# Letting a group's row gathers go on two by two, paced by TensorE's products (graph network layer, one core)

## The chip, the cores and the metric

The kernel runs on one core of one Trainium2 chip. The metric is the device time of one execution in microseconds (us), lower is better. Engines are named as the profile names them: PE is TensorE, DVE VectorE, ACT ScalarE, POOL GpSimd, SP SyncE (it only issues DMAs here).

## What is computed

One message-passing layer of a graph network with a residual and two layer norms: 6250 nodes with 128 features, 100000 edges sorted by destination, 4 attributes an edge.

```python
msg_in = concat([x[src], x[dst], edge_attr], axis=1)     # 100000 x 260
h = silu(msg_in @ mW1 + mb1)
aggregated = segment_sum(h @ mW2 + mb2, dst, num_segments=6250)
u = silu(concat([x, aggregated], axis=1) @ uW1 + ub1)
x = layernorm(x + layernorm(x + u @ uW2 + ub2) * ln_g + ln_b)
```

## The kernel before, in words

The product of `msg_in` with `mW1` is split. A table `tab_a` (all nodes times the first 128 rows of `mW1`) is made once and lies in HBM; `tab_b` is the same for the destinations. The edges are cut into 98 groups of 1024 edges, 8 tiles of 128 each. Since the edges are sorted, the destinations of a group lie in a window of 80 nodes.

One step of the main loop (`for g in range(NG)`, L1005) does one group. For most groups (86 of 98, in the list `listed`; a group's place in that list is its turn) the rows `tab_a[src]` are fetched by indirect DMAs, one for each tile of 128 edges, issued by POOL in `fetch` (L210, the DMA is L215). The other 12 groups (14, 21, 28, ... 91, in `by_sort`) need no gather: TensorE picks their rows from a copy of the table in SBUF with 0/1 matrices (`select`, L938), with products and evictions around it (L915, L916, L924, L945, L953, L954) that are spread over the six steps ahead of such a group.

The step of a listed group g issues, in this order:

- POOL: the gathers of the group four turns ahead (`fetch(ahead(g, 4))`). They go into one of 6 buffers `ga`, so they wait until ACT has read the buffer's last user, the group six turns earlier (L582).
- SP: the loads of the group three turns ahead: destinations (`near`), the window of `tab_b` (`mv`), the attributes (`st`).
- DVE, then ACT: `hidden(g)`: the gathered rows plus the product of the destinations' part (L581, reads `ga` and PSUM `pre`), then SiLU into `h` (L582).
- DVE: the 0/1 matrices of the group two turns ahead (L534 and L544).
- PE: `before_rows` of the next turn's group (L566, 8 tiles, into PSUM `pre`), then what a sorted group ahead needs (L915, L938, L953), then `sums(g)`: a small transpose (L588) and 8 tile products `h` times 0/1 matrix that add up in PSUM `pt` (L590).
- DVE: `add`: `pt` is added to the running sums `acc` and `deg` (L611). There is one buffer `pt`, so the next group's sums wait for it.

Each fp32 product stands in the profile as two matmuls and two weight loads, so a group has 16 records of L566 and 16 of L590. The order on every engine is the order in which the code is written; the waits between engines are semaphores that the framework sets from the tiles. POOL does hardly anything but issue gathers: 40 from `x` for the first five groups, which go another way, and 646 from `tab_a`. Every 512 nodes a batch of the node update (L628 to L690) comes between.

Of the kernel before, what the change touches and what calls it, by code (L numbers as in the profile page):

```python
# [25 lines left out]
def kernel(  # L26
# [18 lines left out]
    nc = tc.nc  # L45
# [5 lines left out]
    G = 8  # L51
# [4 lines left out]
    WS = 112  # L56
# [6 lines left out]
    RAW = 5  # L63
    NM = 4
# [19 lines left out]
    listed = [g for g in range(NG) if g not in by_sort]  # L84
# [7 lines left out]
    def turn_of(g):  # L92
        return listed.index(g)
# [4 lines left out]
    def ahead(g, n):  # L98
        i = listed.index(g) + n
        return listed[i] if i < len(listed) else NG  # L100
# [16 lines left out]
    def tiles_of(g):  # L117
        return min(G, TI - g * G)
# [17 lines left out]
    start = ExitStack()  # L136
    first = start.enter_context(tc.tile_pool(name="first", bufs=1, side="right"))

    def wide():
        return ps.tile([P, G, P], F32, name="pre")  # L140

    def narrow():
        return ps1.tile([P, 2 * P], F32, name="pt")
# [62 lines left out]
    sd = dram.tile([4, QN * GE], F16, name="sd")  # L206
    ea_d = dram.tile([ED, NG * GE], F32, name="ea_d")
    rows, bases, near = {}, {}, {}

    def fetch(g):  # L210
        if g >= NG:
            return
        rows[g] = gath.tile([P, G, H], F32, name="ga")
        for i in range(tiles_of(g)):
            nc.gpsimd.indirect_dma_start(  # L215
                out=rows[g][:, i, :],
                out_offset=None,
                in_=x if g < RAW else tab_a[:, :],
                in_offset=bass.IndirectOffsetOnAxis(ap=src_i[:, g, i : i + 1], axis=0),
            )  # L220

    for g in range(RAW - 1):
        fetch(g)
# [8 lines left out]
    pos_i = first.tile([R, P], I32, name="pos_i")  # L232
    nc.gpsimd.iota(pos_i, pattern=[[P, P]], base=0, channel_multiplier=P * P)
    fetch(RAW - 1)

    b1 = bcast("b1", mb1)
# [165 lines left out]
    def turned_first(k):  # L402
        pt = wide()
        if k < 2:
            turned_x(k, pt, node, name="xT", bufs=3)
        else:
            turned_x(k, pt, first, name="xT", bufs=2)
        return pt

    pt = {0: turned_first(0)}  # L410
# [27 lines left out]
    mv = []  # L438
# [89 lines left out]
    oh, pre, xg, h_s = {}, {}, {}, {}  # L528
# [30 lines left out]
    def before_rows(g):  # L559
        if g >= NG:  # L560
            return
        raw = g < RAW
        pre[g] = wide()
        st = stbuf[turn_of(g) % NST].rearrange("k (i c) -> k i c", i=G)
        for i in range(tiles_of(g)):
            nc.tensor.matmul(pre[g][:, i, :], st[:, i, :], mv[turn_of(g) % NM], start=True, stop=not raw)  # L566
            if raw:
                nc.tensor.matmul(
                    pre[g][:, i, :], xg[g][:, i, :], w1[:, 0, :], start=False, stop=True
                )  # L570
        xg.pop(g, None)
# [12 lines left out]
    def sums(g):  # L584
        n = tiles_of(g)
        h, o = h_s.pop(g) if g in h_s else hbuf[turn_of(g) % 2], oh.pop(g)
        pt = narrow()
        nc.tensor.transpose(pt[0:1, P : P + W], deg_g[:, g : g + 1], ident[:W, :W])  # L588
        for i in range(n):
            nc.tensor.matmul(pt[:, :WS], h[:, i, :], o[:, i, :], start=i == 0, stop=i == n - 1)  # L590
        return pt

    acc, deg = {}, {}
# [57 lines left out]
    def inverse(*parts):  # L651
        r = node.tile([P, 2, 2 * BN], F32, name="r")
        lo, hi = parts[0][0], parts[-1][1]
        nc.scalar.activation(r[:, 0, lo:hi], var[:, lo:hi, 1], AF.Sqrt, bias=eps)
        nc.vector.reciprocal(r[:, 0, lo:hi], r[:, 0, lo:hi])
        nc.vector.scalar_tensor_tensor(
            r[:, 1, lo:hi], var[:, lo:hi, 0], -1.0, r[:, 0, lo:hi], op0=OP.mult, op1=OP.mult
        )
        return r

    def scaled(to, v, r, lo, n):
        for i in range(n):
            nc.scalar.activation(  # L663
                to[:, i, :],
                v[:, i, :],
                AF.Identity,
                bias=r[:, 1, lo + i : lo + i + 1],
                scale=r[:, 0, lo + i : lo + i + 1],
            )
# [11 lines left out]
    def node_o(k, r):  # L681
        i0, n = batches[k]
        o = node.tile([P, BN, H], F32, name="o")
        scaled(o, z_sb.pop(k), r, BN, n)
        m = min(i0 + n, nf) - i0
        if m > 0:
            nc.sync.dma_start(
                out[i0 * P : (i0 + m) * P].rearrange("(i p) f -> p i f", p=P), o[:, :m]
            )
        if i0 + n > nf:  # L690
            nc.scalar.dma_start(out[nf * P :], o[: N - nf * P, nf - i0, :])
# [313 lines left out]
    for g in range(NG):  # L1005
# [14 lines left out]
        if g in by_sort:  # L1020
            select(3)
            sorted_hidden()
            turned_hidden(g, 1)
            add(g, sums(g))
            node_stage(g)
            continue
        if g + AHEAD >= RAW:
            fetch(ahead(g, AHEAD))
        if g < RAW:
            if g + 1 < RAW:  # L1030
                turned_rows(g + 1)
            before_rows(g)
# [6 lines left out]
        if g < SORTED:  # L1039
            n = -(-len(todo) // (SORTED - g))  # L1040
# [3 lines left out]
        if g + 1 >= RAW:  # L1044
            before_rows(ahead(g, 1))
        if g == NG - 1:
            node_x(NB - 1)
        sorted_before(g)
        add(g, sums(g))
        sorted_behind(g)  # L1050
        node_stage(g)
    k = NB - 1
    n = batches[k][1]
# [6 lines left out]
    node_o(k - 1, r)  # L1060
    r = inverse((BN, BN + n))
    node_o(k, r)
    edges.close()
    ub2_b, g_b, b_b = late["ub2"], late["g"], late["b"]

# [100 lines left out]
    with tc.If(bad > 0):  # L1166
        with tc.tile_pool(name="all", bufs=1) as whole:
# [11 lines left out]
            with tc.tile_pool(name="turned", bufs=2, space=PSUM) as turned:  # L1179
                for i in range(NT):  # L1180
                    pt = turned.tile([P, P], F32, name="pt")
# [142 lines left out]
```

## Time and profile before

| | before |
|---|---|
| median of 3 runs | 1409.84 us (1408.27 to 1423.03) |
| the profiled execution | 1407.12 us, its span 1405.3 us |
| PE busy | 888.7 us (63%) |
| POOL busy | 657.3 us (47%), 697 instructions |
| DVE busy | 555.5 us (40%) |
| ACT busy | 368.3 us (26%) |
| granted TensorE clock, mean | 0.786 |

In the groups of instructions a row has the line, the engine, the operation, what is written and read, the count, then busy time and mean duration, then the engine's idle time just before these instructions and what ended most of it. "issue" is idle time that no wait in the profile explains. "remote" is a wait that ended with a semaphore's update for which the profile shows no instruction that ended just then. In a timeline a row has start and duration in us, engine, line, operation, and in brackets the idle time before it.

### The profile page before, as it was taken

How to read it: one execution, taken by the hardware profiler on the slowest of the kernel's cores; microseconds unless marked ns; L12 is line 12 of the kernel's file. 1: busy time of each engine (PE TensorE's matmuls, PEld its weight loads, DVE VectorE, ACT ScalarE, POOL GpSimd, SP SyncE). 2: the span in 40 equal slices, each digit the busy share in tenths (PEclk: the TensorE clock that was granted, in tenths of full speed). 3: DMA queues.
4: the chain of work that ended last, by engine and by line, in shares of the span. 5: the costliest groups of instructions: out<-in, count | busy, mean ns of one | idle time of the engine just before them, and what ended most of it. 6: DMA issues, size and time to landing. Idle time of an engine off the chain costs nothing.

```text
span 1405.3 us, 15177 instructions
## 1 busy us (share of the span) xinstructions
PE 888.7 (63%) x5206; PEld 755.8 (54%) x5206; DVE 555.5 (40%) x1287; ACT 368.3 (26%) x518; POOL 657.3 (47%) x697
## 2 busy tenths in 40 slices
PE   3256738577666657647747757667755864864883
PEld 3246736465564545636636646546545653663672
DVE  1056866343432433533423422342443423443353
ACT  1010103231422323313313311232332412331333
POOL 6434455546444464456264354444555446346310
PEclk9977967787777978868767667868879777786895
DMA  6242324322242322332221421324234232132110
GB/s 176 62 134 79 86 66 116 70 74 73 65 98 63 88 74 74 81 81 72 79 75 43 99 71 42 83 65 99 68 91 90 71 97 72 47 98 67 52 50 19
DMA packets 85950, 109.12 MB, mean 78 GB/s; under 512 B 22044, under 2 KB 63152, under 8 KB 85866
## 3 DMA queue, kind: packets, MB, share of 16 engines
q1 hardware_dynamic: 60114, 61.20, 16.3%
q0 software_dynamic: 21952, 45.00, 13.0%
q10 hardware_dynamic: 3800, 1.88, 0.5%
q8 instruction: 43, 0.70, 0.2%
q14 instruction: 41, 0.34, 0.1%
HBM read 96.65 MB, written 11.37 MB: 77 GB/s over the span
## 4 chain that ended last, share of the span: by engine, by line
PE 34%; another core or an unknown queue 21%; DVE 16%; issue 12%; ACT 7%; DMA 1%; DVEq 1%; POOL 0%; SPq 0%; ACTq 0%
PE pt L590 11%; PE po L938 8%; PE pre L566 5%; DVE ga L581 3%; ACT h L582 2%; DVE st L534 2%; PE po L924 2%; ACT pn L663 1%; DVE bn L622 1%; DVE oh L544 1%; PE pn L636 1%; PE pn L635 1%; PE pn L915 1%; PE pn L953 1%
## 5 line engine op out<-in xcount | busy, mean ns | idle before, releaser
L215 POOL DMA_INDIRECT ga<-tab_a,src_i x646 | 617.8, 956 | 668.3 <-ACT h L582 429.6
L590 PE MATMUL pt<-oh,h 128*128 128x112 f32 x1372 | 230.8, 324 | 146.5 <-ACT h L582 76.5
L590 PEld LDWEIGHTS pt<-oh,h 128*128 128x128 f32 x1372 | 207.0, 232 | 176.2 <-ACT h L582 89.4
L566 PE MATMUL pre<-mv,st 128*128 128x128 f32 x1372 | 214.3, 312 | 27.2 <-issue 18.1
L566 PEld LDWEIGHTS pre<-mv,st 128*128 128x128 f32 x1372 | 202.8, 228 | 42.2 <-issue 30.4
L938 PE MATMUL po<-O,A 128*128 128x157 f32 (+47 forms) x1344 | 196.9, 303 | 34.0 <-issue 33.8
L938 PEld LDWEIGHTS po<-O,A 128*128 128x128 f32 x1344 | 191.5, 214 | 38.7 <-issue 38.4
L582 ACT ACTIVATE h<-ga 128x1024 f32<-128x1024 f32 (+1 forms) x81 | 85.4, 1054 | 353.9 <-DVE ga L581 268.3
L611 DVE TENSOR_TENSOR acc<-acc,pt 128x80 f32 x98 | 23.3, 238 | 384.3 <-PE pt L590 190.7
L534 DVE TENSOR_SCALAR_CACHE_REDUCE st<-near,base_p 80x1024 f32<-80x1024 int32 x86 | 109.0, 1268 | 1.4 <-DMA near<-in_dst_dram 0.8
L581 DVE TENSOR_TENSOR ga<-ga,pre 128x1024 f32<-128x1024 f32 (+1 forms) x81 | 98.3, 1214 | 10.3 <-issue 9.9
L904 ACT ACTIVATE O<-sc,p_less 128x512 f32<-128x512 f16 x96 | 63.5, 709 | 94.9 <-remote 44.8
L916 DVE SCALAR_TENSOR_TENSOR st_s<-ar,part,pn 32x512 f32<-32x512 f16 x24 | 18.1, 756 | 171.3 <-remote 117.5
L924 PE MATMUL po<-st_s,mv_s 128*128 128x512 f32 x48 | 34.5, 808 | 76.1 <-DVE st_s L916 58.6
L544 DVE TENSOR_TENSOR oh<-w_row,rel 128x640 f32<-128x640 f32 x86 | 69.9, 813 | 0.0
L900 DVE TENSOR_SCALAR O<-sc,p_rows 128x512 f32<-128x512 f16 x96 | 44.9, 509 | 44.5 <-remote 32.3
L945 ACT ACTIVATE hT<-po 128x512 f32<-128x512 f32 x24 | 14.3, 594 | 168.8 <-remote 81.3
L905 ACT ACTIVATE O<-O,ones 128x1024 f32<-128x1024 f32 x48 | 55.1, 1149 | 1.6
L924 PEld LDWEIGHTS po<-st_s,mv_s 128*128 128x128 f32 x48 | 9.7, 253 | 81.2 <-DVE st_s L916 62.3
L953 PE MATMUL pn<-ident,hT 128*128 128x128 f32 x96 | 18.8, 328 | 51.5 <-ACT hT L945 35.3
L215 POOL DMA_INDIRECT ga<-in_x_dram,src_i x40 | 37.9, 948 | 14.7 <-issue 11.7
L915 PE MATMUL pn<-Oc,at_s 128*128 128x512 f32 x48 | 33.1, 771 | 16.9 <-issue 9.2
(193 smaller groups left out, 806.6 us busy)
## 6 DMA issues: line engine op xcount, KB each, us to landing
near<-in_dst_dram SPq DMA_DIRECT2D x85, 320.0 KB
ga<-tab_a,src_i POOLq DMA_INDIRECT x646
sc<-sd SPq DMA_DIRECT2D x12, 512.0 KB
mv<-tab_b SPq DMA_DIRECT2D x86, 40.0 KB
tab_a<-A SPq DMA_DIRECT2D x11, 256.0 KB
tab_b<-o SPq DMA_DIRECT2D x11, 256.0 KB
out_dram<-o SPq DMA_DIRECT2D x11, 256.0 KB
x<-in_x_dram SPq DMA_DIRECT2D x10, 256.0 KB
```

Source lines behind the costliest of these rows:

```text
L215: nc.gpsimd.indirect_dma_start(out=rows[g][:, i, :], out_offset=None, in_=x if g < RAW else tab_a[:, :], in_offset=bass.IndirectOffsetOnAx ...
L534: nc.vector.tensor_scalar(stbuf[turn_of(g) % NST][:W], near.pop(g), base_p[:W, g : g + 1], 0.0, op0=OP.is_equal, op1=OP.add, accum_out=deg ...
L544: nc.vector.tensor_tensor(oh[g][:, :n, :W], w_row[:, None, :].to_broadcast([P, n, W]), rel[:, g, :n, None].to_broadcast([P, n, W]), op=OP. ...
L566: nc.tensor.matmul(pre[g][:, i, :], st[:, i, :], mv[turn_of(g) % NM], start=True, stop=not raw)
L581: nc.vector.tensor_add(s[:, :n], s[:, :n], p[:, :n])
L582: nc.scalar.activation(h[:, :n], s[:, :n], AF.Silu)
L590: nc.tensor.matmul(pt[:, :WS], h[:, i, :], o[:, i, :], start=i == 0, stop=i == n - 1)
L904: nc.scalar.activation(O[:, j], key, AF.Square, bias=p_less[:, r : r + 1])
L905: nc.scalar.activation(O[:, 2:], O[:, 2:], AF.Relu, bias=ones[:, 0:1], scale=-1.0)
L915: nc.tensor.matmul(px, t["at"], t["Oc"][:, cols], start=True, stop=True)
L924: nc.tensor.matmul(now["po"], t["mv"], t["st"][:, half * HB : (half + 1) * HB], start=True, stop=False)
L938: nc.tensor.matmul(po[:, lo:hi], A[:, b, :], O[:, b % G - r0, lo:hi], start=False, stop=c % 2 == 1 and i == len(todo) - 1,)
```

## The change

Each gather of an even tile (0, 2, 4, 6) of every paced group gets one more wait, on a product of TensorE; the odd tile behind it goes with it, so the eight gathers of a group go as four pairs. "Paced" are the groups of turn 6 and later (`g > RAW`, 80 groups). For a group of turn t the pairs wait for: tile 0 of `before_rows` of the group of turn t-2, its tile 4, tile 0 of `sums` of the group of turn t-3, its tile 4. These four products stand in one step, that of turn t-3. All other code, the tiles and the order on each engine stay; lines below L215 move down by 1 to 16 (L566 becomes L569, L590 becomes L595).

```diff
+    paced, passed = [], {}
 
     def fetch(g):
 ...
-            nc.gpsimd.indirect_dma_start(
+            ins = nc.gpsimd.indirect_dma_start(
 ...
+            if g > RAW and i % 2 == 0:
+                paced.append((ins, g, i))
 ...
-            nc.tensor.matmul(pre[g][:, i, :], st[:, i, :], mv[turn_of(g) % NM], start=True, stop=not raw)
+            passed["pre", g, i] = nc.tensor.matmul(
+                pre[g][:, i, :], st[:, i, :], mv[turn_of(g) % NM], start=True, stop=not raw
+            )
 ...
-            nc.tensor.matmul(pt[:, :WS], h[:, i, :], o[:, i, :], start=i == 0, stop=i == n - 1)
+            passed["sum", g, i] = nc.tensor.matmul(
+                pt[:, :WS], h[:, i, :], o[:, i, :], start=i == 0, stop=i == n - 1
+            )
 ...
+    for ins, g, i in paced:
+        at = listed[turn_of(g) - 3]
+        key = ("pre", ahead(at, 1), 2 * i) if i < G // 2 else ("sum", at, 2 * i - G)
+        tc.add_manual_dep(
+            ins.ins,
+            passed[key].ins.name,
+            mybir.DependencyInfo(mybir.DependencyClass.Sync, mybir.DependencyReason.DATA),
+            reason="gathers go on with the products",
+        )
```

On POOL, the eight gathers of group 11 before. `DMASW` are the landings of earlier gathers (each gather waits for the one eight before it), `Activation_49` is ACT's signal that the buffer is free.

```order
L215 DMA ga<-tab_a,src_i 128x128 [waits DMASW0_49,Activation_49]
L215 DMA ga<-tab_a,src_i 128x128 [waits DMASW1_49]
L215 DMA ga<-tab_a,src_i 128x128 [waits DMASW2_49]
L215 DMA ga<-tab_a,src_i 128x128 [waits DMASW3_49]
L215 DMA ga<-tab_a,src_i 128x128 [waits DMASW4_49]
L215 DMA ga<-tab_a,src_i 128x128 [waits DMASW5_49]
L215 DMA ga<-tab_a,src_i 128x128 [waits DMASW6_49]
L215 DMA ga<-tab_a,src_i 128x128 [waits DMASW7_49]
```

The same eight gathers on POOL in the changed kernel, where `PE_49` is TensorE's signal:

```order
L216 DMA ga<-tab_a,src_i 128x128 [waits DMASW0_49,PE_49,Activation_49]
L216 DMA ga<-tab_a,src_i 128x128 [waits DMASW1_49]
L216 DMA ga<-tab_a,src_i 128x128 [waits DMASW2_49,PE_49]
L216 DMA ga<-tab_a,src_i 128x128 [waits DMASW3_49]
L216 DMA ga<-tab_a,src_i 128x128 [waits DMASW4_49,PE_49]
L216 DMA ga<-tab_a,src_i 128x128 [waits DMASW5_49]
L216 DMA ga<-tab_a,src_i 128x128 [waits DMASW6_49,PE_49]
L216 DMA ga<-tab_a,src_i 128x128 [waits DMASW7_49]
```

Every second gather has gained a wait for TensorE, and nothing stands in another place.

On PE, the products of the step of group 45 in the changed kernel (`pre` is the product of group 46, L922 the attribute product that was L915, L593 and L595 the sums of group 45, L931 the start of a picked half that was L924):

```order
L569 MATMUL pre<-mv_401,st_483 128x128 [waits DMAHW3_49,DMAHW2_49,DVE_49]
L569 MATMUL pre<-mv_401,st_483 128x128 x7
L922 MATMUL pn<-Oc,at_s 128x512 [waits DMAHW7_49,DVE_49]
L593 MATMUL pt<-ident,deg_g 1x80 [waits DVE_49,PE_49]
L595 MATMUL pt<-oh_487,h_477 128x112 [waits Activation_49]
L595 MATMUL pt<-oh_487,h_477 128x112 x7
L931 MATMUL po<-st_s,mv_s 128x512 [waits DMAHW0_49,DVE_49]
```

These rows are those of before under new line numbers, in the same order with the same waits. The first and fifth tile of L569 open the first two pairs of group 48, and the first and fifth tile of L595 the other two.

## Prediction, made before the changed kernel was run

> **What bounds the kernel now.** First the page. No engine is full, and a third of the chain that ended last is "unknown queue" or "issue", waits that no instruction explains.
>
> ```profile
> span 1405.3 us, 15177 instructions
> PE 34%; another core or an unknown queue 21%; DVE 16%; issue 12%; ACT 7%; DMA 1%; DVEq 1%; POOL 0%; SPq 0%; ACTq 0%
> ```
>
> The view of waits says where the unnamed ones stand (line waited in, who ended it, us in total, times, longest).
>
> ```profile
> POOL ga L215 <- ACT h L582: 429.6, 47, 26.0
> DVE acc L611 <- PE pt L590: 190.7, 43, 15.9
> DVE acc L611 <- remote: 155.5, 21, 15.1
> DVE st_s L916 <- remote: 117.5, 9, 18.8
> ACT hT L945 <- remote: 81.3, 8, 17.5
> ```
>
> All three "remote" rows are instructions that read what PE has just written to PSUM. So I looked at single cases in the timeline (start, duration, instruction, idle time before it).
>
> ```profile
> 697.93 2.04 PE L590 MATMUL pt<-oh,h 128*128 128x112 f32 x16
> 710.53 0.94 POOL L215 DMA_INDIRECT ga<-tab_a,src_i  x1 [0.30 <-issue]
> 714.14 0.24 DVE L611 TENSOR_TENSOR acc<-acc,pt 128x80 f32 x1 [12.78 <-remote]
> 714.67 1.22 DVE L581 TENSOR_TENSOR ga<-ga,pre 128x1024 f32<-128x1024 f32 x1 [0.16 <-issue]
> 715.98 1.06 ACT L582 ACTIVATE h<-ga 128x1024 f32<-128x1024 f32 x1 [15.69 <-DVE ga L581]
> 717.09 3.75 PE L590 MATMUL pt<-oh,h 128*128 128x112 f32 x16 [2.13 <-ACT h L582]
> 717.30 0.94 POOL L215 DMA_INDIRECT ga<-tab_a,src_i  x1 [5.83 <-ACT h L582]
> 720.88 0.24 DVE L611 TENSOR_TENSOR acc<-acc,pt 128x80 f32 x1 [1.14 <-PE pt L590]
> 736.02 0.94 POOL L215 DMA_INDIRECT ga<-tab_a,src_i  x1 [0.30 <-issue]
> 740.09 0.76 DVE L916 SCALAR_TENSOR_TENSOR st_s<-ar,part,pn 32x512 f32<-32x512 f16 x1 [15.53 <-remote]
> 963.61 0.94 POOL L215 DMA_INDIRECT ga<-tab_a,src_i  x1 [4.08 <-ACT h L582]
> 965.27 3.71 PE L938 MATMUL po<-O,A 128*128 128x19 f32 x30
> 972.34 0.94 POOL L215 DMA_INDIRECT ga<-tab_a,src_i  x1 [0.30 <-issue]
> 974.97 0.60 ACT L945 ACTIVATE hT<-po 128x512 f32<-128x512 f32 x1 [11.16 <-remote]
> 980.38 0.24 DVE L611 TENSOR_TENSOR acc<-acc,pt 128x80 f32 x1 [14.53 <-PE pt L590]
> ```
>
> The sums of 697.93 end at 699.97 by PE's record, yet DVE takes them at 714.14: 14.2 us late, and 2.7 us after a run of gathers ended (710.53 + 0.94 = 711.47). At 740.09 it is 3.1 us after the end of the next run (736.96). The picked half ends at 968.98, and ACT takes it at 974.97, 1.7 us after that run ended (973.28). Against these stands 720.88: sums that end 3.5 us into a run (begun 717.30) are taken within 0.04 us. My reading: **PE's results come through in the first 4 us or so of a run of gathers, then they are held until POOL has paused for 1.7 to 3.1 us**, 2.5 in the mean of these three.
>
> A stretch inside a run against one without gathers (us, then busy time and count of PE, PEld, DVE, ACT and POOL, granted clock, DMA share, GB/s), and the free steps themselves:
>
> ```profile
> 721.30:737.00 15.70, 9.86 (x59) 7.84 (x58) 3.15 (x4) 1.06 (x1) 12.01 (x13) 0.82 0.30 82
> 1347.70:1362.90 15.20, 12.64 (x101) 11.84 (x100) 10.83 (x20) 3.17 (x3) 0.00 (x0) 0.95 0.15 44
> 1347.75 0.24 DVE L611 TENSOR_TENSOR acc<-acc,pt 128x80 f32 x1 [5.56 <-PE pt L590]
> 1352.72 0.24 DVE L611 TENSOR_TENSOR acc<-acc,pt 128x80 f32 x1 [1.29 <-PE pt L590]
> 1357.69 0.24 DVE L611 TENSOR_TENSOR acc<-acc,pt 128x80 f32 x1 [1.29 <-PE pt L590]
> ```
>
> 59 matmuls in 15.7 us under gathers, 101 in 15.2 us without, and a step then takes 5.0 us. So DVE, ACT and PE wait for each other only because PE's signals wait for POOL's pauses, and POOL pauses only when its six buffers are full.
>
> **POOL's account.** I count in the stretch of 11 equal rounds of seven steps (from 305.0, behind sorted group 14, to 1347.7, behind group 91).
>
> ```profile
> 305.00:1347.70 1042.70, 503.58 (x526) 0.78 0.30 75
> POOL ga L215 <- ACT h L582: 382.0, 41, 26.0
> POOL ga L215 <- issue: 147.1, 476, 1.6
> POOL ga L215 <- DVE st L534: 7.0, 1, 7.0
> POOL ga L215 <- DMA ga<-tab_a,src_i: 2.4, 8, 0.3
> ```
>
> (The first row is POOL's gathers alone, the others POOL's waits there.) 526 gathers, 66 groups, take 503.6 + 147.1 = 650.7 us, 1.24 us each, 9.9 a group. Stops take 382.0 + 7.0 + 2.4 = 391.4 us. Gathering can't shrink; the change moves the stops.
>
> **The change, part by part.** *Where a pair now starts.* The run at 717.30 begins group 52. Its gates are in the step of group 48:
>
> ```profile
> 750.96 1.95 PE L566 MATMUL pre<-mv,st 128*128 128x128 f32 x16
> 762.89 1.97 PE L590 MATMUL pt<-oh,h 128*128 128x112 f32 x16
> 807.99 1.22 DVE L581 TENSOR_TENSOR ga<-ga,pre 128x1024 f32<-128x1024 f32 x1 [0.15 <-issue]
> ```
>
> The pairs, 2.5 us apart from 717.30 on, would start 32 to 41 us later by these products (tiles 0 and 4 of each), so the gates do bite and ACT's wait no longer does. DVE needs the rows at 807.99, still 44 us behind the last gate; at the new pace two steps lie between, at least 10 us, for 2.5 us of issuing. Behind a waiting gather POOL holds only further gathers, and only DVE's L581 waits for those.
>
> *What a stop costs.* Before, after a release the way back to POOL is L611, L581 and L582: 717.30 - 714.14 = 3.2 us, and often a second step has to pass as well: 41 stops of 382.0 / 41 = 9.3 us. Now the releaser is PE itself. When POOL pauses, PE's held signals come through together, those of the sums and of the next `pre` (issued behind them): up to four pairs are open at once. DVE, ACT and PE then do the next step inside the run, 3.2 us plus 2.0 of sums, too late for the first 4 us, so their result is held again. I take one release of 2.5 us for each group: 66 x 2.5 = 165 us. A sorted step opens no pairs; undisturbed it takes 3.7 us (L938) plus 980.38 - 974.97 = 5.4, 9.1 in all: 11 x 9.1 = 100 us. Together 265 against 391: **126 us less, 1.9 a group.**
>
> *The beginning.* The same 1.9 us for the groups gathered ahead of 305:
>
> ```profile
> 150.00:305.00 155.00, 76.42 (x81) 0.77 0.31 81
> ```
>
> 81 gathers, ten groups: 19 us less.
>
> *The end.* Before, gathering is over when the last six steps begin (this row again POOL alone):
>
> ```profile
> 1347.70:1405.30 57.60, 0.00 (x0) 0.74 0.08 23
> ```
>
> Now groups 95, 96 and 97 are gathered in the steps of 92, 93 and 94, which go from 5.0 to 9.9 + 2.5 = 12.4 us: 22 us more.
>
> *Edits at nothing.* PE's four signals a step are parts of matmuls that are there. A wait that needs an instruction of its own on POOL costs 17 ns (median of the row), 319 of them 5 us; POOL's stops hide them, and without that cover they are the price.
>
> ```profile
> L215 POOLq EVENT_SEMAPHORE  x84: 17/17/25277, 46.0 to 1320.9; - x84
> ```
>
> *Sum.* 1405.3 - 126 - 19 + 22 = 1282; the execution was 1.8 us above its span (1407.12), so **1284 us**. That execution lies 2.7 below the median of 1409.84, so I compare within 0.2%.
>
> *The price of a release from both sides.* At 1.7 us: stops 112 + 100, a gain of 179, 27 at the beginning, 20 lost at the end: 1221. At 3.1: stops 305, a gain of 86, 13 at the beginning, 25 lost: 1333. What the extra signals do to PE while they are held no row shows. Free is one end; the other is that PE stops at the first one held, and its `pre` (1.95 us, row 750.96) moves behind the release, where 3.2 us of DVE and ACT cover it: also nothing, as long as the sums are done. I take nothing.
>
> The Trainium skill, "SBUF — State Buffer", section "Who interferes with whom", says that PE never waits for anyone and that a DMA never contends with a compute engine. The rows 59 against 101 matmuls don't agree, unless something else than SBUF's ports holds PE. By that rule alone the sum would be 1407, the second rival below.
>
> **The rivals.** (1) *Slower: two stops a group.* The first two pairs are 5 us of gathers, longer than the 4 us that signals get through. If the sums' signals are always held, POOL runs dry behind pair two, stops 2.5 us, does the other two and stops again: 66 x 5 + 100 = 430 us against 391, 39 more, 6 more at the beginning, 3 x (9.9 + 5 - 5.0) = 30 more at the end: **1482 us**. It decides from (391 - 100) / (66 x 2.5) = 1.8 stops a group. For it: in select steps 3.7 us of L938 stand between `pre` and sums. Against: each stop also moves the step on, and what PE did in the meantime opens more than two pairs.
>
> (2) *No change: the gathers aren't the cause.* Runs and held results could both follow from a third thing, say PE's own slow stretches. POOL then only fetches later what isn't needed yet: **1407 us**. For it: the longest waits fall in the longest runs, and a slow step lets POOL fetch more. Against: three releases at 1.7 to 3.1 us behind a run's end.
>
> (3) *Much faster: pauses between pairs are enough.* If holding never sets in, the stops in groups go: 391 - 100 = 291 us less, 44 at the beginning, 3 x (9.9 - 5.0) = 15 lost: 1087, which POOL's own work then bounds; a release now and then gives **1090 to 1220**.
>
> (4) *The change does nothing,* if POOL is so far behind that the gates are open: excluded while steps are slower than 9.9 us a group; after that it is case 3's bound.
>
> **How the numbers follow.** One stop a group, 1221 to 1333: 0.45. From there to 1393 (1% below), more than one stop and less than 1.8: 0.06. Case 3: 0.15. Case 2: 0.13. Case 1: 0.21. Faster by over 1% (what a measurement of this kernel can tell) is 0.66, within it 0.13, slower 0.21. The range 1190 to 1450 leaves out about 0.06 of case 3 and 0.14 of case 1, whose lower third is 1.8 to 1.9 stops a group.
>
> **What would show it.** POOL's row "<- ACT h" gone, one "<- PE" in its place with about 80 stops near 3 us; the "remote" rows of L611, L916 and L945 shorter, none over 13 us; no run over ten gathers; the steps of groups 92 to 94 near 12 us. Twice as many stops is case 1; "remote" rows unchanged with gathers spread out is case 2. Most wrong would make me a hold that begins with the first gather, since then every pair costs its own release.

## The result, and the profile after

| | before | changed |
|---|---|---|
| median, side by side, 4 runs each | 1416.43 us (1408.27 to 1429.99) | 1254.53 us (1246.26 to 1259.17) |
| the profiled execution, its span | 1407.12 us, 1405.3 us | 1252.3 us, 1250.5 us |

The ratio is 0.890, with an interval of 0.886 to 0.893: 11% faster. Forecast were 1284 us and a range of 1190 to 1450.

One thing has to be known for all that follows: the kernel before took 1393 to 1430 us in some sessions and 929 to 949 us in others, with nothing between, so each ratio is taken against the kernel before in its own session. I call them long and short sessions; the table is from long sessions. The ratios leave out runs of over 1.5% above the fastest of their kernel, so they differ by up to 0.4% from the quotient of the medians.

The page of the changed kernel, its span and its chain:

```profile
span 1250.5 us, 15414 instructions
PE 48%; DVE 15%; issue 15%; another core or an unknown queue 9%; ACT 7%; DMA 3%; ACTq 1%; SPq 1%; POOL 0%; DVEq 0%
```

The unknown part of the chain fell from 21% to 9%, and PE's rose from 34% to 48%. The view of waits, over the whole span:

```profile
POOL ga L216 <- issue: 288.1, 576, 14.0
DVE acc L618 <- PE pt L595: 151.2, 32, 10.9
DVE acc L618 <- remote: 80.5, 14, 12.1
POOL ga L216 <- PE pt L595: 76.7, 43, 5.2
DVE st_s L923 <- remote: 46.9, 8, 10.6
ACT hT L952 <- remote: 44.6, 7, 9.9
```

The three "remote" rows, results of PE that came through late, are 155.5, 117.5 and 81.3 us before and 80.5, 46.9 and 44.6 us now. One kind of stop looks like this in the timeline:

```profile
726.71 0.94 POOL L216 DMA_INDIRECT ga<-tab_a,src_i  x1 [0.30 <-issue]
729.65 1.11 POOL L216 DMA_INDIRECT ga<-tab_a,src_i  x1 [2.00 <-remote]
730.37 0.24 DVE L618 TENSOR_TENSOR acc<-acc,pt 128x80 f32 x1
738.56 0.95 POOL L216 DMA_INDIRECT ga<-tab_a,src_i  x1 [0.30 <-issue]
738.57 1.75 PE L595 MATMUL pt<-oh,h 128*128 128x112 f32 x14
741.19 0.37 PE L595 MATMUL pt<-oh,h 128*128 128x112 f32 x2 [0.87 <-issue]
741.68 0.95 POOL L216 DMA_INDIRECT ga<-tab_a,src_i  x1 [2.17 <-PE pt L595]
743.29 0.24 DVE L618 TENSOR_TENSOR acc<-acc,pt 128x80 f32 x1
746.10 1.98 PE L595 MATMUL pt<-oh,h 128*128 128x112 f32 x16
750.64 0.94 POOL L216 DMA_INDIRECT ga<-tab_a,src_i  x1 [0.30 <-issue]
753.46 0.24 DVE L618 TENSOR_TENSOR acc<-acc,pt 128x80 f32 x1 [0.66 <-remote]
753.52 0.94 POOL L216 DMA_INDIRECT ga<-tab_a,src_i  x1 [1.94 <-remote]
```

POOL gathers eight times (729.65 to 739.51), stops 2.17 us, gathers eight times (741.68 to 751.58), stops 1.94 us, and goes on. The sums begun at 746.10 end by their record at 748.08, 6.4 us into a run, and DVE takes them at 753.46, 1.9 us behind that run's end. So holding has not gone; POOL now stops after 6.9 gathers in the mean of the stretch below (528 in 77 runs; 25 of the runs have eight and 24 have four) instead of 12.5 (526 in 42).

The stretch of the 11 rounds, from the sums of group 14 to those of group 91, and what is left behind it (POOL's gathers alone; us, then busy time and count, granted clock, DMA share, GB/s):

```profile
290.10:1170.80 880.70, 509.12 (x528) 0.84 0.34 89
1170.80:1250.50 79.70, 20.81 (x22) 0.67 0.12 35
```

Rounds: 1042.7 to 880.7, 162 us less. Beginning: 305.0 to 290.1, 15 less. End: 57.6 to 79.7, 22 more. Together 155, the difference of the two spans. The pauses of POOL of more than 0.9 us in the stretch were 42, in sum 381 us, with a median of 7.7 us; they are now 77, in sum 225 us, with a median of 2.2.

### The profile page after: what moved, and what is told of

It reads as the page before. It is cut to its first block, busy times and chain, and to the rows that moved or that the text cites. A ratio compares the mean times of both kernels' runs of the same rounds, so it can differ in the third digit from the quotient of the medians.

```text
span 1250.5 us, 15414 instructions
## 1 busy us (share of the span) xinstructions
PE 866.2 (69%) x5206; PEld 744.6 (60%) x5206; DVE 553.9 (44%) x1287; ACT 368.7 (29%) x518; POOL 661.6 (53%) x697
## 4 chain that ended last, share of the span: by engine, by line
PE 48%; DVE 15%; issue 15%; another core or an unknown queue 9%; ACT 7%; DMA 3%; ACTq 1%; SPq 1%; POOL 0%; DVEq 0%
PE pt L595 15%; PE po L945 11%; PE pre L569 8%; DVE ga L586 3%; PE po L931 2%; ACT h L587 2%; PE pn L922 2%; DVE st L537 2%; DVE po L774 2%; ACT pn L670 1%; PE pre L387 1%; PE pn L387 1%; ACTq L587 1%; PE pn L960 1%
## 5 line engine op out<-in xcount | busy, mean ns | idle before, releaser
L595 PE MATMUL pt<-oh,h 128*128 128x112 f32 x1372 | 236.3, 337 | 131.0 <-ACT h L587 68.1
L595 PEld LDWEIGHTS pt<-oh,h 128*128 128x128 f32 x1372 | 217.6, 245 | 155.6 <-ACT h L587 77.7
L569 PE MATMUL pre<-mv,st 128*128 128x128 f32 x1372 | 211.9, 311 | 19.8 <-DVE xg L560 10.7
L569 PEld LDWEIGHTS pre<-mv,st 128*128 128x128 f32 x1372 | 202.4, 227 | 35.4 <-issue 21.3
L945 PE MATMUL po<-O,A 128*128 128x157 f32 (+47 forms) x1344 | 184.6, 296 | 13.0 <-issue 12.9
L945 PEld LDWEIGHTS po<-O,A 128*128 128x128 f32 x1344 | 181.5, 206 | 14.0 <-issue 14.0
L618 DVE TENSOR_TENSOR acc<-acc,pt 128x80 f32 x98 | 23.3, 238 | 327.6 <-PE pt L595 151.2
L931 PE MATMUL po<-st_s,mv_s 128*128 128x512 f32 x48 | 36.4, 849 | 29.7 <-issue 11.6
L952 ACT ACTIVATE hT<-po 128x512 f32<-128x512 f32 x24 | 14.3, 596 | 136.7 <-PE po L945 58.9
L923 DVE SCALAR_TENSOR_TENSOR st_s<-ar,part,pn 32x512 f32<-32x512 f16 x24 | 18.1, 756 | 81.9 <-remote 46.9
L593 PE MATMUL pt<-ident,deg_g 80*1 80x80 f32 x98 | 24.4, 249 | 30.3 <-DVE deg L618 16.6
L922 PE MATMUL pn<-Oc,at_s 128*128 128x512 f32 x48 | 31.7, 736 | 14.5 <-issue 7.4
L380 PE MATMUL pre<-ident,xf 128*128 128x128 f32 x41 | 8.7, 345 | 47.2 <-issue 39.9
```

Of the source, the lines that this page charges most:

```text
L569: passed["pre", g, i] = nc.tensor.matmul(pre[g][:, i, :], st[:, i, :], mv[turn_of(g) % NM], start=True, stop=not raw)
L595: passed["sum", g, i] = nc.tensor.matmul(pt[:, :WS], h[:, i, :], o[:, i, :], start=i == 0, stop=i == n - 1)
L922: nc.tensor.matmul(px, t["at"], t["Oc"][:, cols], start=True, stop=True)
L931: nc.tensor.matmul(now["po"], t["mv"], t["st"][:, half * HB : (half + 1) * HB], start=True, stop=False)
L945: nc.tensor.matmul(po[:, lo:hi], A[:, b, :], O[:, b % G - r0, lo:hi], start=False, stop=c % 2 == 1 and i == len(todo) - 1,)
```

## The experiments

My theory as it stood in the prediction: runs of gathers hold PE's results, and the change gains because POOL's stops are shorter and come in time. Rivals: POOL's being at work holds them, gathers or not; the gathers have nothing to do with it; the gain is from fetching later, not from PE's signals; the gain is from PE's signal at the group's start, not from the pairs. The lengths of steps and pauses below are counted from the traces as in the two stretches above; a run of gathers is one without a pause of over 0.9 us.

### First session, a short one: the kernel before at 941.17 us (932.65 to 944.62, 13 runs)

**plain_loads**

```diff
         for i in range(tiles_of(g)):
-            ins = nc.gpsimd.indirect_dma_start(...)
+            if g > RAW:
+                t0 = (g * G + i) % (NT - 1) * P
+                nc.sync.dma_start(rows[g][:, i, :], tab_a[t0 : t0 + P, :])
+                continue
+            nc.gpsimd.indirect_dma_start(...)
```

> The kernel before, but the rows of every group of turn 6 and later are not gathered: SP loads as many contiguous rows of tab_a in their place (eight loads of 128 rows a group, the same 45 MB in all with the first groups, 512 bytes a row), so the rows are other ones and POOL has nothing to do. Theory (POOL's gathers hold PE's results): the rounds of seven steps fall from 94.8 us to between 45 and 65, the time to 880 to 1080 us, and no instruction waits over 5 us for a result that PE's records had finished. Rival (the traffic of rows into SBUF holds PE, whoever issues it): rounds stay above 85 us, 1300 us or more. Rival (PE's slow stretches come from neither): about 1405.

952.39 us, a ratio of 1.015 (1.008 to 1.021). Taken alone, that says that the gathers cost nothing. It doesn't answer the question, since here the kernel before itself took 470 us less than in the session of the prediction.

**pool_memsets**

```diff
+            if g > RAW:
+                nc.gpsimd.memset(rows[g], float(i))
+                continue
```

> The kernel before, but each gather of a group of turn 6 and later is replaced by a POOL memset of the group's whole buffer (128 x 1024), so the rows are constants: POOL works about as long, with no DMA. Theory (it takes the gathers' DMAs, not POOL at work): 880 to 1080 us like plain loads, with POOL's busy time still above 300 us. Rival (POOL being busy is enough): runs of memsets hold PE as runs of gathers do, and the time stays above 1300 us.

942.75 us, 1.002 (0.998 to 1.007). POOL was busy for 686 us, 74% of the span, and nothing was held. Since nothing was held under gathers either in that session, it doesn't tell what POOL at other work does in a long one.

**one_gate**

```diff
-            if g > RAW and i % 2 == 0:
+            if g > RAW and i == 0:
                 paced.append((ins, g, i))
```

> The changed kernel with a wait on the first gather of a group alone (tile 0 of the product two turns ahead of it); the other seven follow at once. Theory (what counts is that POOL starts from PE's own signal, one release a step): runs of eight as in the changed kernel, between 1230 and 1290 us. Rival (the pairs spread the gathers and that keeps PE going): the gain falls by half or more, over 1330 us. Splitting could also cost stops: then 1200 to 1235.

948.93 us, 1.011 (1.003 to 1.018). Here its trace is worth more than its time. POOL's waits in the whole span (the 44.1 us are one wait ahead of the rounds), its gathers in the 11 rounds, and one case in the timeline:

```profile
POOL ga L216 <- issue: 202.2, 646, 4.5
POOL ga L216 <- PE pre L569: 45.9, 7, 44.1
218.20:888.10 669.90, 505.27 (x527) 0.93 0.46 117
619.25 1.97 PE L595 MATMUL pt<-oh,h 128*128 128x112 f32 x16
621.06 0.95 POOL L216 DMA_INDIRECT ga<-tab_a,src_i  x1 [0.30 <-ACT O L912]
621.26 0.24 DVE L618 TENSOR_TENSOR acc<-acc,pt 128x80 f32 x1 [0.23 <-PE pt L595]
622.31 0.95 POOL L216 DMA_INDIRECT ga<-tab_a,src_i  x1 [0.30 <-issue]
```

527 gathers in 670 us, 1.27 us each, 428 of them in one run without a pause. In the midst of it DVE takes sums 0.04 us after their record ends (621.22). No sums of this trace wait longer than 7.6 us, against 17.5 us before. So gathers do not hold PE's results in every session. Here POOL never pauses in the run of 428, so its pace is the bound: 48 gathers a round at 1.26 us are 60.5 us, and a round takes 60.9. The rest is hardly faster: in pool_memsets, which gathers nothing in the rounds, a round takes 60.1.

**act_gate**

```diff
-        nc.scalar.activation(h[:, :n], s[:, :n], AF.Silu)
+        passed["h", g] = nc.scalar.activation(h[:, :n], s[:, :n], AF.Silu)
 ...
-        key = ("pre", ahead(at, 1), 2 * i) if i < G // 2 else ("sum", at, 2 * i - G)
+        key = ("h", at)          # and one gate a group, as in one_gate
```

> The changed kernel with one wait a group, on ACT's SiLU of the group three turns ahead in place of PE's products: gathers are as late as in the changed kernel, but POOL starts from the end of the way PE, DVE, DVE, ACT, as before the change. Theory (the gain is the way that POOL no longer waits for): most of the gain goes, 1370 to 1450 us (before plus about 22 at the end). Rival (gathers that are issued later, in smaller heaps, are the gain, whoever opens them): 1240 to 1300 us.

951.05 us, 1.014 (1.008 to 1.020), again with a run of over 400 gathers. So one gate a group costs about 1% in a short session. The end, whose last groups are fetched later, takes 65.5 us against 57.5 in pool_memsets, which has no gates. That is 8 us; the median lies 10 us above that of the kernel before. In one_gate the end takes 60.9, so there it explains only part of the 8 us.

### Second session, a long one: the kernel before at 1410.06 us (1392.77 to 1420.6, 13 runs)

**before_again** and **after_again** are the two kernels unchanged.

> The kernel before, unchanged, for its trace on this chip. Where it takes about 940 us: POOL's wait for ACT gone or below 100 us, a round of seven steps at 60 to 62 us (POOL's 48 gathers), sums that are taken late by over 8 us in none of the 98 steps, though runs of gathers are longer than 20. Where it takes about 1410: as in the first profile.

> The changed kernel, unchanged, beside the kernel before on one chip. In the last four runs the kernel before took 941 us on chip 2, not 1410, and no result of PE was held. Theory A (holding is a condition of some chips, and the change gains only there): where the kernel before takes about 1410 us, 0.88 to 0.90 of it; where it takes about 940, 1.00 to 1.03 of it, since gates can only make POOL wait and the last three groups' gathers come later. Rival B (the change is worth its 11% anywhere): below 0.93 of the kernel before on every chip.

1407.66 us, and 1233.93 us (1224.75 to 1238.6), a ratio of 0.872 (0.865 to 0.879). The gain stands; it is larger here than in the first comparison, and the two intervals don't meet, so a per cent or two hangs on the session. The trace of before_again shows the holding again: 12 sums are taken over 8 us late. Theory A's "condition of some chips" falls, since this is the chip that took 941 us in the first session.

**plain_loads_2**, the edit of plain_loads:

> As plain_loads (contiguous rows loaded by SP in place of the gathers, so other rows), for the chip's condition. Where the kernel before takes about 1410 us: theory (POOL's gathers hold PE) 930 to 1080 us; rival (any traffic of rows holds it) over 1250; rival (PE is slow there whatever is fetched) over 1350. Where it takes about 940: 940 to 960 again.

991.88 us, 0.703 (0.697 to 0.709). The windows of the 11 rounds, without gathers in the long session, without them in the short one, and with them in the long one (this row of before_again); the columns as in the prediction, PE, PEld, DVE, ACT, POOL:

```profile
255.40:935.20 679.80, 568.95 (x4045) 498.68 (x4044) 385.91 (x804) 300.35 (x419) 0.00 (x0) 0.93 0.43 116
```

```profile
214.80:890.20 675.40, 566.86 (x4046) 496.46 (x4045) 385.99 (x804) 300.38 (x419) 0.00 (x0) 0.93 0.42 116
```

```profile
304.60:1347.90 1043.30, 681.11 (x4044) 577.24 (x4043) 388.60 (x804) 299.39 (x419) 504.65 (x526) 0.77 0.29 75
```

Without gathers a round is the same in both sessions (61.8 and 61.4 us); with them it takes 94.8 us in the long one. The granted clock goes the same way, 0.93 without gathers and 0.77 with them; waits of over 10 us behind sums of 2 to 4 us are not explained by it. Only the beginning still differs, 255 us against 215 to the end of group 14, and there the first groups' gathers remain. All of the 40 us are lost before the first group's sums are taken (123.1 against 82.5 us), while the table is made under the first 40 gathers (4.7 to 55.1 us, with a pause of 0.9 us at 44.5):

```profile
20.31 0.69 DVE L403 COPY A<-pre 128x512 f32<-128x512 f32 x1 [5.98 <-remote]
45.55 0.69 DVE L403 COPY A<-pre 128x512 f32<-128x512 f32 x1 [18.75 <-remote]
61.00 0.69 DVE L403 COPY A<-pre 128x512 f32<-128x512 f32 x1 [14.76 <-remote]
```

In the short session no DVE wait there is longer than 4.0 us. So the 400 us are the gathers' in a long session: the rival without them falls. What of them is needed (the indirect DMA, the scattered rows, or just any work of POOL) isn't shown by this, since all three went.

**act_gate_2**, the edit of act_gate:

> As act_gate (one wait a group, on ACT's SiLU three turns ahead). Where the kernel before takes about 1410 us: theory (the way back to POOL is the gain) 1370 to 1450; rival (late gathers in heaps of eight are the gain) 1240 to 1300. Where it takes about 940: 945 to 960 again.

1424.74 us (1415.94 to 1429.18), 1.013 (1.009 to 1.018). Its waits of POOL in the 11 rounds:

```profile
POOL ga L216 <- ACT h L587: 394.5, 43, 23.2
POOL ga L216 <- issue: 144.7, 474, 0.6
```

As before the change: stops of 9.2 us, runs of 8 (22 times), 16 (16) and 24 (4). The groups are fetched as late as in the changed kernel, the end is as long (79.5 us), and nothing is gained. So fetching later isn't what gains; what releases POOL is.

### Third session, a short one: the kernel before at 936.52 us (928.87 to 948.78, 12 runs)

**pool_pause** and **spaced_pairs** give POOL pauses that hang on no signal, filled by memsets of buffers that the gathers then write.

```diff
         rows[g] = gath.tile([P, G, H], F32, name="ga")
+        if g > RAW:                              # pool_pause
+            for _ in range(3):
+                nc.gpsimd.memset(rows[g], 0.0)
         for i in range(tiles_of(g)):
+            if g > RAW and i % 2 == 0:           # spaced_pairs, instead
+                for _ in range(4):
+                    nc.gpsimd.memset(rows[g][:, i : i + 2, :], 0.0)
```

> The kernel before, without gates, but POOL clears the group's buffer three times (3 memsets of 0.95 us) before it gathers into it: a pause of about 3 us ahead of each group of turn 6 and later, in which POOL works but no gather is issued. Where the kernel before takes about 1410 us: theory (held results come through 1.7 to 3.1 us after the gathers pause, so one pause a group is what the change gives) 12.9 us a group step, 87 a round, 1250 to 1350 us, though POOL does more. Rival (the gates matter because PE opens them, a blind pause is no use): 1400 to 1500. Where it takes about 940, POOL is the bound and the pause is added: 1080 to 1150.

> The kernel before, without gates, but with four small POOL memsets (about 1.2 us together) ahead of every second gather: as much POOL time as pool_pause and a little more, cut into four short pauses a group. Where the kernel before takes about 1410 us: theory (a pause has to last 1.7 us or more to let results through) no gain, 1380 to 1550 us. Rival (what counts is how densely gathers follow on average, a backlog that fills and drains): below 1330 us. Where it takes about 940: 1180 to 1280, POOL's time alone.

pool_pause took 1139.18 us (1137.12 to 1141.02), 1.217 (1.205 to 1.228), as expected where nothing is held: POOL's own time. spaced_pairs took 1407.12 us (1405.68 to 1408.34), 1.503 (1.489 to 1.517), far off the mark. POOL in both timelines, pool_pause first:

```profile
589.98 2.98 POOL L216 MEMSET ga<- 128x1024 f32 x3
593.24 0.95 POOL L218 DMA_INDIRECT ga<-tab_a,src_i  x1 [0.27 <-POOL ga L216]
```

```profile
601.07 1.44 POOL L217 MEMSET ga<- 128x256 f32 x4
602.89 0.95 POOL L218 DMA_INDIRECT ga<-tab_a,src_i  x1 [0.39 <-POOL ga L217]
604.15 0.95 POOL L218 DMA_INDIRECT ga<-tab_a,src_i  x1 [0.30 <-issue]
605.10 1.43 POOL L217 MEMSET ga<- 128x256 f32 x4
606.92 0.95 POOL L218 DMA_INDIRECT ga<-tab_a,src_i  x1 [0.39 <-POOL ga L217]
```

A pair takes 606.92 - 602.89 = 4.03 us, of which the memsets and the gap behind them are 1.8; four pairs are 16.1 us and a round of six such groups 97, measured 98.7. I had put the small memsets too low. That its time comes near that of the long sessions is chance: POOL is its bound, and no sums waited longer than 7.2 us. Neither kernel tells of holding.

**one_gate_2**, the edit of one_gate:

> As one_gate (the changed kernel with a wait on the first gather of a group alone). Where the kernel before takes about 1410 us: theory (POOL's start from PE's own signal, with a release a step) 1200 to 1290 us, within 4% of the changed kernel's 1234. Rival (the pairs are the gain): over 1330. Where it takes about 940: 945 to 955 again.

947.41 us (941.73 to 953.37), 1.013 (1.008 to 1.018), as in the first session.

### Fourth session, a long one: the kernel before at 1408.96 us (1396.78 to 1417.6, 7 runs)

**one_gate_3**, the edit of one_gate:

> Changed kernel, but only the first of a group's four pairs waits for PE (tile 0 of the pre product two turns back); the other seven gathers follow without a wait. The same edit gave 1.011 and 1.013 of the kernel before where that took about 940 us. What is still open is a session in which the kernel before takes about 1410 us. There: if it is POOL's start from PE's own signal that gains, whatever the size of the run, 0.86 to 0.91 of the kernel before (1210 to 1285 us), with runs of mostly 8 and 16 gathers. If the pairs are what gains, because a run of eight or more holds PE's results, 0.97 to 1.02 (1370 to 1440 us), like the kernel whose groups wait for ACT three turns back. Where the kernel before takes about 940 us, both give 1.01 (945 to 955 us) and nothing is told apart.

1338.79 us (1330.06 to 1350.54), 0.947 (0.939 to 0.954): between the two expectations, and neither. The timeline shows both halves:

```profile
703.12 1.97 PE L595 MATMUL pt<-oh,h 128*128 128x112 f32 x16
706.88 0.94 POOL L216 DMA_INDIRECT ga<-tab_a,src_i  x1 [0.31 <-issue]
709.54 0.24 DVE L618 TENSOR_TENSOR acc<-acc,pt 128x80 f32 x1 [4.64 <-remote]
710.29 0.95 POOL L216 DMA_INDIRECT ga<-tab_a,src_i  x1 [2.46 <-issue]
712.43 2.04 PE L595 MATMUL pt<-oh,h 128*128 128x112 f32 x16 [1.16 <-ACT h L587]
714.61 0.24 DVE L618 TENSOR_TENSOR acc<-acc,pt 128x80 f32 x1 [0.54 <-PE pt L595]
729.13 0.95 POOL L216 DMA_INDIRECT ga<-tab_a,src_i  x1 [0.30 <-issue]
733.18 0.59 ACT L961 COPY h_s<-pn 128x512 f32<-128x512 f32 x1 [14.00 <-remote]
752.47 0.94 POOL L216 DMA_INDIRECT ga<-tab_a,src_i  x1 [22.39 <-issue]
```

The first stop, behind the run that ends at 707.82, is 2.46 us, short because, by the code, PE's own signal lifts it (the profile names no releaser). But the next run goes on from 710.29 to 730.08, sixteen gathers, because the second group's gate was open by the time the first group was through; ACT's copy of another product of PE then waits 14.0 us and comes 3.1 us behind the run's end, and POOL stands for 22 us. The long sessions side by side, counted from the traces between the sums of group 14 and of group 91 (one_gate_3's trace is of an execution of 1350.54 us, 12 us above its median, so its row is rough by that much):

| kernel | ratio | 11 rounds, us | POOL's runs | pauses: sum, median | group step, sorted step | end |
|---|---|---|---|---|---|---|
| before_again | 1 | 1043 | 42 | 381, 8.1 | 13.9, 11.3 | 57.9 |
| act_gate_2 (ACT, once a group) | 1.013 | 1047 | 42 | 384, 7.7 | 14.1, 10.6 | 79.5 |
| one_gate_3 (PE, once a group) | 0.947 | 966 | 50 | 298, 3.6 | 13.2, 8.7 | 73.2 |
| after_again (PE, four pairs) | 0.872 | 869 | 76 | 215, 2.2 | 11.7, 9.1 | 75.7 |
| plain_loads_2 (no gathers) | 0.703 | 680 | none | none | 8.9, 8.2 | 57.2 |

Between act_gate_2 and one_gate_3 only the signal differs: 81 us of the rounds. Between one_gate_3 and after_again only the pairs: 97 us. The sums of pauses fall by 86 and 83. So PE's signal and the pairs each bring about half of the gain, by the rounds as by the ratios (1.013, 0.947, 0.872).

## Why the prediction was right, and where not

**The mechanism** (held results, a release when POOL pauses): it holds for long sessions in the main. The timelines show it again in changed kernels, with releases 1.7 us (709.54 against 707.82) and 1.9 us behind a run's end, and taking the gathers away ends it. The rule was read from three releases, and not every late result waits for a pause of 1.7 to 3.1 us. Of the 14 sums that are taken over 8 us late in the first profile, seven come 2.4 to 3.1 us behind the end of their run, five come 3.7 to 5.5 us behind it, and two come while the run goes on. One of these two, in a run of 24 gathers from 591.93 to 622.16:

```profile
609.04 0.24 DVE L611 TENSOR_TENSOR acc<-acc,pt 128x80 f32 x1 [8.92 <-remote]
621.22 0.94 POOL L215 DMA_INDIRECT ga<-tab_a,src_i  x1 [0.30 <-issue]
```

What the prediction could not see is that the stall isn't part of the kernel: one_gate's code, which stalls in the fourth session, ran 428 gathers on end in the first with nothing held. It never asked whether the stall would be there in another session.

**The rounds,** -126 forecast, -162 measured. The step that failed is "I take one release of 2.5 us for each group". A group's step was to take 9.9 + 2.5 = 12.4 us and took 11.74: 44 us over 66 steps. The count was about right (77 stops in the stretch, "about 80" forecast); the size was not: a median of 2.2 us instead of 2.5, in the lower part of the 1.7 to 3.1 that three releases had shown. The gathers themselves take what was forecast, 880.7 - 225.5 = 655 us, or 1.24 us each. A sorted step took 9.62 us, 9.1 forecast: 6 us the other way. 44 - 6 is 38, against 36 missing; the rest is rounding (9.86 taken as 9.9 us a group).

**The beginning,** -19 forecast, -15 measured. **The end,** +22 forecast, +22.1 measured; yet the steps of groups 92, 93 and 94, forecast near 12 us each, took 6.7, 9.5 and 15.8, so only their sum was right.

**The signs.** ACT's row of POOL's waits, 382.0 us in the stretch before, should go; a remnant stays:

```profile
POOL ga L216 <- issue: 225.1, 434, 14.0
POOL ga L216 <- PE pt L595: 72.0, 39, 5.2
POOL ga L216 <- remote: 28.1, 15, 3.0
POOL ga L216 <- ACT h L587: 5.3, 3, 2.5
```

Its place is taken by PE's, as said, but not in one row: much of it stands as "issue", which was 147.1 us before; the profile names no releaser for those stops. The "remote" rows of L618, L923 and L952 are shorter, the longest 12.1 us, "none over 13" forecast. "No run over ten gathers" was wrong: three runs have twelve, and a stretch from 1014 to 1036 us has only one pause near 1 us in sixteen gathers. It begins right behind a sorted step (the pause ahead of it is 5.3 us); that this step had opened the gates ahead is likely, not shown.

**The rivals.** Two stops a group (1482 us) came in a minority: counted group by group, 50 of the 66 had one stop, 14 had two and 2 had none (78, with the one that is under way as the stretch begins), 1.2 in the mean where the rival needed 1.8. That pauses between pairs let nothing be held (1090 to 1220 us) is wrong too: six times in the span sums are still taken over 8 us late, up to 10.9. That gathers aren't the cause fell with plain_loads_2. The Trainium skill, "SBUF — State Buffer", section "Who interferes with whom", from which 1407 us followed, has a side that the prediction did not see: in a short session the trace agrees with it (one_gate, sums taken at once amid 428 gathers), in a long one it does not (1043 against 680 us for the rounds with and without gathers), unless, as the prediction has it, something else than SBUF's ports holds PE.

**What stays open.** What makes a session long or short; the kernels don't, since the same ones ran in both. What lets a late result through: a pause of POOL is the usual case, not the only one. Whether PE's results are held or its products are done later than recorded: the ends of PE's records are modelled, so the traces can't tell the two apart. Whether another work of POOL would hold PE's results in a long session: the memsets ran in a short one only. How the changed kernel with its four pairs stands in a short session: only one gate a group ran there, at 1.011 and 1.013, so a small loss is to be reckoned with. No version tried beats the changed kernel with the same results in a long session.

## What to carry to other kernels

Where an engine takes results long after the other's record has ended, lay the runs of a third engine's DMAs beside them: here the profile's "remote" and "unknown" waits were the only trace of a stall of 360 us in the rounds. If a stall can't be taken away, two things make it cheaper: let the stalled engine's own signal lift it rather than one that is two engines further on, and cut the work that causes it into pieces small enough that it can't run ahead through a second opening. Run the kernel before again in every session, and look whether the stall is there at all, before a saving or a loss is put down to an edit.

## What the runs showed of the hardware that was not expected

The same kernel with the same data took 1410 us in one session and 941 and 937 us in others; the difference goes with the gathers, since a round without any takes 61.8 us and 61.4. In the short sessions a POOL that issues a gather every 1.26 us without a pause holds nothing back. In the long sessions results of PE that end more than about 4 us into a run mostly come through late, in the first profile half of the 14 latest sums 2.4 to 3.1 us after the run and two of them within it. Three POOL memsets of 128x1024 took 2.98 us, four of 128x256 1.44 us, 0.99 and 0.36 us each: a quarter of the elements costs over a third of the time, with some 0.3 to 0.4 us more before the next gather starts.
